# An edge-gated graph layer on one core: GpSimd's queue keeps only fetches and value gathers, SyncE's takes the rest

## The chip, the cores and the metric

The kernel runs on one core of a Trainium2 chip. The metric is the device time of one execution in microseconds (us); the time before is 1040.96 us, the median of three runs (1038.32 to 1042.02).

Names as in the profile: PE is TensorE (matrix products), DVE is VectorE, ACT is ScalarE, POOL is GpSimd, SP is SyncE. SP only issues DMAs. Each engine takes its instructions strictly in the order of the program, so an instruction that waits holds up all that stand behind it on that engine.

## The reference

One layer of a graph network over 16 batches, 1024 nodes and 256 features, with one sparse adjacency matrix for all batches (about 0.8% of entries, and the diagonal):

```python
pre_u = jnp.einsum('bud,dk->buk', h_t, W1[:d])
pre_v = jnp.einsum('bvd,dk->bvk', h_t, W1[d:])
hidden = jax.nn.relu(pre_u[:, :, None, :] + pre_v[:, None, :, :] + b1)
S = jax.nn.sigmoid(jnp.einsum('buvk,ko->buvo', hidden, W2)[..., 0] + b2[0])
a_t = jnp.einsum('buv,bud->bvd', S * A_a, h_t)
m_t = jnp.einsum('uv,bud->bvd', A_m, h_t) * h_t
z_t = beta1 * h_t + beta2 * (a_t @ Wa + ba) + beta3 * (m_t @ Wm + bm)
```

`A_a` and `A_m` are the same matrix `adj`. The last line is shortened from two einsums. Only pairs (u, v) with an edge matter, so the kernel lists the edges and works on these.

## The kernel before, in words

**Blocks and steps.** The 16 batches form four groups of four (`NG`, `GB`). The 1024 target nodes form eight tiles of 128 (`NT`). One group and one tile make a block: 32 blocks, and each is done in ten steps (`T`), so 320 steps in all. Blocks run in a fixed `order`: tiles 0 to 5 of group 0, tiles 0 to 5 of group 1, tiles 6 and 7 of both, then groups 2 and 3. Group 1's table is thus first needed at block 6, by step 60.

**Lists.** For each tile a list of edges is made (`lists(vt)`, line 236). It loads a 128x1024 piece of the adjacency into `key` (line 238), finds the neighbours with DVE's top-8 instruction, computes a matrix of marks on ACT (`mark`, lines 305 to 307), copies it to bytes as `few` (lines 310 and 312), and writes it out with four DMAs to `whose` (line 315), which the blocks read later. It leaves row numbers `uidx` for the fetches and `vidx` for the gathers of edge values. Lists 0 to 3 are made in the opening, the end of list 3 in the first steps; lists 4 to 7 start at steps 7, 14, 44 and 82 and are threaded between the steps' instructions.

**Tables.** For each group a table in device memory holds, for each node, 4x256 values of `pre_u` beside 4x256 values of `h`: 8 KB a row. A piece of rows is made by `rows(k)` (line 429): PE multiplies a transposed tile of x (`hT`, 0.5 MB, `load_hT` at line 400) by `w_u`, ACT copies the result to `tab`, SP writes it to the table. `copy_h` (line 406) copies the `h` half from memory to memory. Group 0's table is made in the opening. Group 1's eight tiles follow in steps that `plan` lists at line 806, two pieces to a tile; `made_rows(n)` (line 813) loads a tile ahead of its first step, when one of the few places in `hT_free` is open, and makes the piece when its step comes.

**A step.** `fetch(n)` (line 513) is an indirect DMA on POOL: 128 edges, one 8 KB table row each, 1 MB in all, into one of eight places (`fetched`). PE spreads `pre_v` over the edges (`expand`, line 616). DVE adds it (`add`, line 646) and, batch by batch, takes the relu, multiplies by W2 and sums (`gate`, line 653). ACT makes the sigmoid (line 656) and scales the edge weights (line 660). PE sums the fetched `h` rows per target (`aggregate`, line 669). Then the place is free and the next fetch is issued, with one or two gathers of edge values (`fetch_val`, line 356), one DMA of 128 numbers each. The products with `Wa` and `Wm` and the output follow at the end of a block.

**The order of the work** is written out by hand. The opening is a `script` (line 544) of 14 short strings: a digit advances that list, `r` makes rows, `h` the first block's `pre_v`, `f` issues the first eight fetches and five value gathers, `w` warms PE up, `m` loads the first mark. After it comes the loop over steps. `after(step, f)` runs `f` at the end of that step. POOL's queue, in the part that matters here, holds: fetches 0 to 7 with five gathers and two `hT` loads among them (in `f`); then `key` of list 4, `w_a`, `w_m`; then the four `whose` writes of list 2; then one `hT` load, the four `whose` writes of list 3, and only then fetch 8.

**Bias.** In step 1 SP loads the biases and the betas; in step 10 `scale_late` (line 598) scales them with seven DVE instructions, and the two weight matrices with two ACT instructions.

Of the kernel before, what the change touches and what calls it, by code (L numbers as in the profile page):

```python
# [11 lines left out]
ALU = mybir.AluOpType  # L12
AX = mybir.AxisListType
P = 128
# [3 lines left out]
def kernel(  # L18
# [42 lines left out]
    nc = tc.nc  # L61
    B, N, D = x.shape
    NT = N // P
    DC = D // P
# [3 lines left out]
    W = 64  # L68
    NW = P // W
# [31 lines left out]
    def fixed(shape, name, dt=FP):  # L101
        return const.tile(shape, dt, name=name)
# [74 lines left out]
    def spread(parts, v):  # L177
        nc.vector.tensor_copy(parts, v)
        nc.vector.tensor_tensor(parts[W:], v[W:], parts[W:].bitcast(FP), ALU.subtract)
        nc.vector.tensor_scalar(parts, parts.bitcast(FP), edge, None, ALU.mult)  # L180

    b1_p = fixed([P, D], "b1_p", FR)
    bias_p = fixed([P, D], "bias_p", FR)
# [5 lines left out]
    whose = const.tile([P, NT * NW, E], mybir.dt.uint8, name="whose")  # L189
# [31 lines left out]
    EARLY = 4  # L221
# [13 lines left out]

    def lists(vt):
        key = fetched[vt + 1][:, :N] if vt < EARLY else lst.tile([P, N], FP, name="key", bufs=1)
        (nc.sync if vt < EARLY else nc.gpsimd).dma_start(key, adjT[vt * P:(vt + 1) * P, :])
        yield "load"
        R = Rs[vt % EARLY]  # L240
        top = R[:, 4:]
# [64 lines left out]
        nc.scalar.activation(mark, mark, AF.Sign, bias=span[:, 0:1], scale=-1.0)  # L306
        nc.scalar.activation(mark, mark, AF.Relu)
        yield "step"
        if vt < EARLY:
            nc.scalar.copy(few, mark)  # L310
        else:
            nc.gpsimd.tensor_copy(few, mark)
        for w in range(NW):
            for h in range(2):
                nc.gpsimd.dma_start(whose[h * W:(h + 1) * W, vt * NW + w, :], few[w * W:(w + 1) * W])
        pe = aside(vt)
        for j in range(TW):
            nc.tensor.matmul(pe[:, j * NW * RC:(j + 1) * NW * RC], mark[:, j * P:(j + 1) * P],
# [54 lines left out]
    def after(step, f):  # L373
        due.setdefault(step, []).append(f)
# [8 lines left out]
    hTs = {}  # L383
# [16 lines left out]
    def load_hT(k, engine=nc.sync):  # L400
        g, nt = k
        hTs[k] = hT_free.pop(0)
        engine.dma_start(hTs[k].rearrange("p b c n -> p (b c) n"),
                         xT_rows[:, g * GB * DC:(g + 1) * GB * DC, nt * P:(nt + 1) * P])
# [95 lines left out]
    T = TW * NW  # L500
# [40 lines left out]
    for i in range(COPIES):  # L541
        copy_h(turn[i], nc.sync)

    script = ("r r 0 0", "r r 1 0 0", "r r 1", "r 0 0", "r r 1", "0 2 r 1", "0 0 r r", "1 2 r 1", "v r r 2", "r 1 3",
              "h 2 1 1", "h 2 2 3", "f 2 2 2 w h h h", "m 3 w 3 3 3")
    begun_rows = {}
    marks, pcs, accs, evs, hbs, LTs, lefts = {}, {}, {}, {}, {}, {}, {}

# [4 lines left out]
    def warm(times):  # L553
        acc = psa.tile([P, 2, D], FP, name="acc")
        for i in range(times):
            nc.tensor.matmul(acc, unit, b1_p.unsqueeze(1).to_broadcast([P, 2, D]), start=True, stop=True)

    m = 0
    piece = None
    parts = halves(0)  # L560
    for t, turns_ in enumerate(script):
        step = t - 100
        do(step)
        for c in turns_.split():
            if c == "r":
                k = turn[m % NT]
                if m < NT:
                    begun_rows[k] = rows(k, tabs[m])
                    next(begun_rows[k])
                go(begun_rows[k], step)  # L570
                if m > NT and m - NT + COPIES <= NT:
                    copy_h(turn[m - NT + COPIES - 1], nc.sync)
                m += 1
            elif c == "h":
                go(parts, step)
            elif c == "v":
                fetch_val(3)
                spread(b1_p, b1_b)
                next(parts)
            elif c == "f":  # L580
                for n in range(NF):
                    fetch(n)
                    if n > 2:
                        fetch_val(1)
                    if n in (3, 6):
                        load_hT(turn[NT + n // 6], nc.gpsimd)
                next(made[EARLY])
                w_a = load_weights(Wa, "w_a", nc.gpsimd)
                w_m = load_weights(Wm, "w_m", nc.gpsimd)
            elif c == "m":  # L590
                load_mark(0)
            elif c == "w":
                warm(6)
            else:
                next(made[int(c)], None)
    do(len(script) - 100)

    def scale_late():
        nc.vector.tensor_scalar(ba_b, ba_b, be2, None, ALU.mult)
        nc.vector.scalar_tensor_tensor(bias, bias, be3, ba_b, ALU.mult, ALU.add)  # L600
        spread(bias_p, bias)
        nc.vector.tensor_scalar(ba_c, ba_c, be2, None, ALU.mult)
        nc.vector.scalar_tensor_tensor(bias_c, bias_c, be3, ba_c, ALU.mult, ALU.add)
        nc.scalar.activation(w_a, w_a, AF.Copy, scale=be2)
        nc.scalar.activation(w_m, w_m, AF.Copy, scale=be3)
        hT_free.append(spare_)

# [192 lines left out]
    def plan(blocks, ns):  # L800

        for k, pieces in zip(blocks, ns):
            pending.append((pieces[0], k))
            at.update((n, k) for n in pieces)

    plan(turn[NT:], ((2, 4), (8, 9), (10, 15), (19, 20), (25, 29), (30, 35), (39, 40), (45, 47)))
    for g, first in ((2, 60), (3, 140)):
        plan([(g, vt) for vt in range(NT)], ((first + 9 + 10 * i, first + 14 + 10 * i) for i in range(NT)))
    pending.extend((order.index(k) * T - T + 1, k) for k in again)
# [2 lines left out]

    def made_rows(n):
        nonlocal piece, last
        while pending and (pending[0][1] in hTs or hT_free and pending[0][0] - AHEAD <= n):
            k = pending.pop(0)[1]
            if k not in hTs:
                load_hT(k, nc.gpsimd if n < T else nc.sync)
        if n in at:
            if at[n] != last:  # L820
                last = at[n]
                copy_h(last, nc.sync)
                piece = rows(last)
                next(piece)
            go(piece, n)
# [58 lines left out]
    for n in range(total - 3):  # L884
        k, s = divmod(n, T)
        if n < ROOM:
            gather_to(n - 1)
        pair_ends()
        if n % TW == (n < ROOM) and n // TW + 1 < total // TW:
            load_mark(n // TW + 1)  # L890
        expand(n + 2)
        if n >= ROOM:
            fill(n, False)
        products(n, k, s)
        if n >= ROOM and n % 2 == 0:
            gather_to(n)
        add(n + 1)
        gate(n)
        while behind:
            nc.scalar.copy(*behind.pop(0))  # L900
        do(n)
        if n == 1:
            bias = load_rows(bm, D, "bias", nc.sync, spare[:, 1])
            ba_b = load_rows(ba, D, "ba_b", nc.sync, spare[:, 2])
            bias_c, ba_c = fixed([P, DC], "bias_c"), fixed([P, DC], "ba_c")
            nc.sync.dma_start(bias_c, bm.rearrange("(c p) -> p c", p=P))
            nc.sync.dma_start(ba_c, ba.rearrange("(c p) -> p c", p=P))
            be1 = load_rows(beta1, 1, "be1", nc.sync)
            be2 = load_rows(beta2, 1, "be2", nc.sync)
            be3 = load_rows(beta3, 1, "be3", nc.sync)  # L910
            after(10, scale_late)
        if n == total - 6:
            hbs[BS - 1] = next(t for t in hT_free if t in flat).rearrange("p b c n -> p b (c n)")
            for v, m, f in tails:
                for h, o in tail_rows(x, v, m, f):
                    nc.sync.dma_start(h, o)
        for i in advance.get(n, ()):
            next(made[i], None)
        if n in start_list:
            running.append([made[start_list[n]], True, n])  # L920
            piece_of(running[-1], n)
        if n < ROOM:
            fill(n, False)
        if n == LISTS:
            assert not running and all(next(x, None) is None for x in made)
            lists_done()
            more = main.enter_context(tc.tile_pool(name="more", bufs=1))
            flat.extend(hT_places(more, MORE, NH))
            hT_free.extend(flat[-MORE:])
            minus.append(more.tile([P, P], FR, name="minus"))  # L930
            nc.vector.tensor_scalar(minus[0], ident, -1.0, None, ALU.mult)
        if n == 120:
            nc.vector.tensor_tensor(rest, rest, taken, ALU.subtract)
            nc.gpsimd.partition_all_reduce(longest, rest, P, bass_isa.ReduceOp.max)
            after(n + 12, count_rest)
# [152 lines left out]
```

## Time and profile before

| what | value |
|---|---|
| median of three runs | 1040.96 us |
| the profiled execution | 1031.14 us, span 1029.3 us |
| DVE busy | 950.4 us (92%) |
| PE busy | 958.9 us (93%) |
| ACT busy | 886.5 us (86%) |
| POOL busy | 467.5 us (45%) |
| moved by DMA | 375.00 MB, mean 364 GB/s |

The span runs from the first to the last of the program's instructions. An engine's idle time is shown before the instruction that ended it, in square brackets, with what it waited for. "remote" means that the profile cannot name the releaser. POOL's DMAs are those of queue 0 (software), SP's those of queue 1 (hardware). The "DMA share" is the mean busy share of the core's 16 DMA engines; as packets of two queues overlap, it can go a little above 1.

### The profile page before, as it was taken

The page shows a single profiled execution, that of the slowest core. Times are in us where ns is not written, and L with a number is a line of the kernel's source. Part 1 is how long each engine was busy: PE and PEld are TensorE (multiplying, and loading weights), DVE is VectorE, ACT ScalarE, POOL GpSimd, SP SyncE. Part 2 cuts the span into 40 slices and gives each one's busy share as a digit, 9 for nine tenths or more (in the row PEclk, how much of TensorE's full clock was granted, in tenths as well). Part 3 has the DMA queues.
Part 4 walks back from the last instruction along what each step waited for, and adds up shares of the span by engine and source line. Part 5 has one row for each costly group of instructions (what it writes and reads, how often), then busy time and mean ns, then how long its engine had stood idle before and what let it go on. Part 6 is the DMA issues. An engine that isn't in the chain of part 4 may idle for free.

```text
span 1029.3 us, 21645 instructions
## 1 busy us (share of the span) xinstructions
PE 958.9 (93%) x6408; PEld 700.3 (68%) x6408; DVE 950.4 (92%) x3302; ACT 886.5 (86%) x2750; POOL 467.5 (45%) x487
## 2 busy tenths in 40 slices
PE   7886789999899999999999999999999999999996
PEld 5754566676567766767677777777777766777663
DVE  7585979988999999998999999999999999999994
ACT  3665777888888989989899999999999999999984
POOL 3367676746246433564333334333343344444430
PEclk9988899999999999999999999999999999999998
DMA  9898998999999999999999999999999999999992
GB/s 326 304 371 305 350 327 287 332 382 343 360 330 334 378 412 392 381 355 391 411 412 408 414 403 413 401 404 408 391 418 390 379 370 364 381 362 378 373 360 73
DMA packets 123199, 375.00 MB, mean 364 GB/s; under 512 B 17616, under 2 KB 76496, under 8 KB 86864
## 3 DMA queue, kind: packets, MB, share of 16 engines
q0 software_dynamic: 50976, 302.73, 76.1%
q1 hardware_dynamic: 71472, 70.27, 20.3%
q8 instruction: 53, 0.87, 0.3%
q10 hardware_dynamic: 624, 0.52, 0.2%
q14 instruction: 74, 0.61, 0.1%
HBM read 377.53 MB, written 50.33 MB: 416 GB/s over the span
## 4 chain that ended last, share of the span: by engine, by line
PE 45%; DVE 28%; issue 12%; ACT 7%; DMA 5%; POOL 2%; another core or an unknown queue 1%; POOLq 0%; DVEq 0%; SPq 0%; ACTq 0%
DVE fetched L653 15%; PE misc L414 13%; DVE fetched L646 11%; PE misc L740 9%; PE pc L616 8%; PE acc L669 8%; PE misc L691 4%; DMA fetched<-table,uidx 3%; ACT left L660 2%; POOL fetched L516 2%; DVE LT L708 1%; PE misc L724 1%; DMA val<-in_adjT_dram,vidx 1%; DMA wide<-in_xT_dram 1%; DVE low L477 1%
## 5 line engine op out<-in xcount | busy, mean ns | idle before, releaser
L516 POOL DMA_INDIRECT fetched<-table,uidx x320 | 342.7, 1071 | 464.6 <-PE acc L669 318.9
L653 DVE SCALAR_TENSOR_TENSOR fetched<-fetched,w_b 128x256 f32<-128x256 f32 x1280 | 476.7, 425 | 0.0
L646 DVE TENSOR_TENSOR fetched<-fetched,pc 128x1024 f32<-128x1024 f32 x320 | 389.8, 1218 | 43.0 <-DMA fetched<-table,uidx 13.8
L660 ACT ACTIVATE left<-left,gt 128x16 f32<-128x16 f32 x1280 | 285.7, 298 | 0.0
L616 PE MATMUL pc<-X,mark 128*128 128x512 f32 x640 | 227.5, 450 | 21.6 <-DVE fetched L646 17.3
L669 PE MATMUL acc<-fetched,left 128*32 128x256 f32 x2560 | 189.9, 388 | 13.0 <-ACT gt L656 4.5
L616 PEld LDWEIGHTS pc<-X,mark 128*128 128x128 f32 x640 | 105.9, 190 | 108.9 <-issue 55.0
L669 PEld LDWEIGHTS acc<-fetched,left 128*32 128x32 f32 x2560 | 74.4, 109 | 92.9 <-issue 30.0
L656 ACT ACTIVATE gt<-sc,b_b 128x4 f32<-128x4 f32 x320 | 96.7, 302 | 39.4 <-DVE fetched L653 31.6
L740 PE MATMUL misc<-w_a,LT 128*128 128x256 f32 x496 | 117.6, 380 | 1.6 <-issue 1.0
L740 PE MATMUL misc<-w_m,LT 128*128 128x256 f32 x496 | 117.3, 380 | 0.0
L653 DVE DVE_READ_ACCUMULATOR fetched<-fetched,w_b 128x1 f32 x1280 | 108.7, 85 | 0.0
L740 PEld LDWEIGHTS misc<-w_a,LT 128*128 128x128 f32 x496 | 93.8, 190 | 16.6 <-issue 1.4
L677 ACT COPY ev<-acc 128x512 f32<-128x512 f32 x160 | 92.2, 577 | 9.8 <-PE misc L414 5.2
L414 PE MATMUL misc<-w_u,wide 128*128 128x256 f32 x384 | 93.4, 392 | 7.2 <-DMA w_u<-in_W_dram 7.1
L624 ACT ACTIVATE left<-onehot,val 128x32 f32<-128x32 bf16 x320 | 99.9, 312 | 0.0
L356 POOL DMA_INDIRECT val<-in_adjT_dram,vidx x80 | 84.9, 1062 | 26.2 <-issue 21.0
L740 PEld LDWEIGHTS misc<-w_m,LT 128*128 128x128 f32 x496 | 89.7, 191 | 9.7
L691 PE MATMUL misc<-ident,ev 128*128 128x128 f32 x642 | 82.8, 274 | 7.1 <-ACT ev L677 3.0
L414 PE MATMUL misc<-w_v,wide 128*128 128x256 f32 x368 | 88.4, 384 | 0.0
L414 PEld LDWEIGHTS misc<-w_u,wide 128*128 128x128 f32 x384 | 74.7, 197 | 19.8 <-DMA w_u<-in_W_dram 7.1
L691 PEld LDWEIGHTS misc<-ident,ev 128*128 128x128 f32 x642 | 74.0, 141 | 17.1 <-ACT ev L677 4.1
(167 smaller groups left out, 1007.6 us busy)
## 6 DMA issues: line engine op xcount, KB each, us to landing
table<-in_x_dram SPq DMA_DIRECT2D x32, 512.0 KB
out_dram<-z SPq DMA_DIRECT2D x62, 256.0 KB
table<-tab SPq DMA_DIRECT2D x48, 256.0 KB
wide<-in_xT_dram SPq DMA_DIRECT2D x16, 512.0 KB
fetched<-table,uidx POOLq DMA_INDIRECT x320
wide<-in_xT_dram SPq DMA_DIRECT2D x4, 1024.0 KB
table<-fetched SPq DMA_DIRECT2D x8, 512.0 KB
hT<-in_xT_dram SPq DMA_DIRECT2D x8, 512.0 KB
```

Of the source, the lines that this page charges most:

```text
L414: nc.tensor.matmul(p[:, bb * D:(bb + 1) * D], hT[:, 2 * h + bb, i, :], wt[:, i, :], start=(i == 0 and not begun), stop=(i == DC - 1), skip ...
L516: nc.gpsimd.indirect_dma_start(out=fetched[at_slot[n]], out_offset=None, in_=table[g], in_offset=bass.IndirectOffsetOnAxis(ap=uidx[:, vt * ...
L616: nc.tensor.matmul(pcs[n][:, c], marks[n // TW][:, j * P:(j + 1) * P], cuts[k][w][:, c], start=True, stop=True)
L624: nc.scalar.activation(lefts[n][:, 1::GB, :], onehot[:, vt * NW + w, j, :].unsqueeze(1).to_broadcast([P, GB // 2, V]), AF.Copy, scale=val[ ...
L646: nc.vector.tensor_tensor(t, t, pcs.pop(n), ALU.add)
L653: nc.vector.scalar_tensor_tensor(t[:, b, :], t[:, b, :], 0.0, w2_b, ALU.max, ALU.mult, accum_out=sc[:, b:b + 1])
L656: nc.scalar.activation(gt, sc, AF.Sigmoid, bias=b2_b)
L660: nc.scalar.activation(lefts[n][:, 2 * b, :], lefts[n][:, 1 + b // 2 * GB, :], AF.Copy, scale=gt[:, b:b + 1])
L669: nc.tensor.matmul(accs[i][b * 2 * V:(b + 1) * 2 * V, r, :], left[:, 2 * b - b % 2:2 * b - b % 2 + 2].rearrange("p k v -> p (k v)"), f[:, ...
L677: nc.scalar.copy(evs[i], accs.pop(i))
L691: nc.tensor.matmul(pt[:, :, FROM[j]:FROM[j] + V], evs[i][:, r, c * P:(c + 1) * P], ident, is_transpose=True, start=(j == of[0]), stop=True ...
L740: nc.tensor.matmul(pz[:, bb * D:(bb + 1) * D], LT[:, 2 * h + bb, i if bb else 1 - i, c, :], wt[:, c, :], start=(i == 1 and bb == 0 and c = ...
```

## The change

All DMAs on POOL but the indirect ones move to SP: `key` of lists 4 to 7, all 32 `whose` writes, the early `hT` loads, `w_a` and `w_m`. The byte copy `few` of lists 4 to 7 moves from POOL to ACT.

The biases and betas are loaded in the opening, at `f`, and scaled at the end of the opening (`scale_bias`, `s` in the script); the spare place that held them is given to `hT_free` there, and not in step 10. The weights are still scaled in step 10.

The first `hT` tile of group 1 is loaded at `k` in the script, the second at the end of step 0, behind the `whose` writes of list 3 and ahead of `key`, `w_a` and `w_m`. Later ones come 6 steps ahead of their first piece while the step is under 10, and 14 steps ahead after that, as before. The pieces themselves fall in steps whose last digit is 1, 3, 8 or 9 (but for the first two, in steps 4 and 6), from step 4 to 41, where they fell in steps 2 to 47.

```diff
-        (nc.sync if vt < EARLY else nc.gpsimd).dma_start(key, adjT[vt * P:(vt + 1) * P, :])
+        nc.sync.dma_start(key, adjT[vt * P:(vt + 1) * P, :])
...
-        if vt < EARLY:
-            nc.scalar.copy(few, mark)
-        else:
-            nc.gpsimd.tensor_copy(few, mark)
+        nc.scalar.copy(few, mark)
         for w in range(NW):
             for h in range(2):
-                nc.gpsimd.dma_start(whose[h * W:(h + 1) * W, vt * NW + w, :], few[w * W:(w + 1) * W])
+                nc.sync.dma_start(whose[h * W:(h + 1) * W, vt * NW + w, :], few[w * W:(w + 1) * W])
...
-              "h 2 1 1", "h 2 2 3", "f 2 2 2 w h h h", "m 3 w 3 3 3")
+              "h 2 1 1", "h 2 2 3", "f 2 2 2 k w h h h", "m 3 w 3 3 3 s")
...
+    def scale_bias():
+        nc.vector.tensor_scalar(ba_b, ba_b, be2, None, ALU.mult)
+        nc.vector.scalar_tensor_tensor(bias, bias, be3, ba_b, ALU.mult, ALU.add)
+        spread(bias_p, bias)
+        nc.vector.tensor_scalar(ba_c, ba_c, be2, None, ALU.mult)
+        nc.vector.scalar_tensor_tensor(bias_c, bias_c, be3, ba_c, ALU.mult, ALU.add)
+        hT_free.append(spare_)
...
                     fetch(n)
                     if n > 2:
                         fetch_val(1)
-                    if n in (3, 6):
-                        load_hT(turn[NT + n // 6], nc.gpsimd)
-                next(made[EARLY])
-                w_a = load_weights(Wa, "w_a", nc.gpsimd)
-                w_m = load_weights(Wm, "w_m", nc.gpsimd)
+                bias = load_rows(bm, D, "bias", nc.sync, spare[:, 1])
...
+            elif c == "k":
+                load_hT(turn[NT])
+            elif c == "s":
+                scale_bias()
...
-    plan(turn[NT:], ((2, 4), (8, 9), (10, 15), (19, 20), (25, 29), (30, 35), (39, 40), (45, 47)))
+    plan(turn[NT:], ((4, 6), (9, 11), (13, 18), (19, 21), (23, 28), (29, 31), (33, 38), (39, 41)))
...
-        while pending and (pending[0][1] in hTs or hT_free and pending[0][0] - AHEAD <= n):
+        while pending and (pending[0][1] in hTs or hT_free and pending[0][0] - (AHEAD if n >= T else 6) <= n):
...
-                load_hT(k, nc.gpsimd if n < T else nc.sync)
+                load_hT(k, nc.sync)
...
+        if n == 0:
+            for i in advance[0]:
+                next(made[i], None)
+            load_hT(turn[NT + 1])
+            next(made[EARLY])
+            w_a, w_m = load_weights(Wa, "w_a", nc.sync), load_weights(Wm, "w_m", nc.sync)
+            after(10, scale_weights)
```

More of the change, by code (lines that the diff above doesn't have):

```diff
@@ L584 @@
                         fetch_val(1)
-                    if n in (3, 6):
-                        load_hT(turn[NT + n // 6], nc.gpsimd)
-                next(made[EARLY])
-                w_a = load_weights(Wa, "w_a", nc.gpsimd)
-                w_m = load_weights(Wm, "w_m", nc.gpsimd)
+                bias = load_rows(bm, D, "bias", nc.sync, spare[:, 1])
+                ba_b = load_rows(ba, D, "ba_b", nc.sync, spare[:, 2])
+                bias_c, ba_c = fixed([P, DC], "bias_c"), fixed([P, DC], "ba_c")
+                nc.sync.dma_start(bias_c, bm.rearrange("(c p) -> p c", p=P))
+                nc.sync.dma_start(ba_c, ba.rearrange("(c p) -> p c", p=P))
+                be1 = load_rows(beta1, 1, "be1", nc.sync)
+                be2 = load_rows(beta2, 1, "be2", nc.sync)
+                be3 = load_rows(beta3, 1, "be3", nc.sync)
+            elif c == "k":
+                load_hT(turn[NT])
+            elif c == "s":
+                scale_bias()
             elif c == "m":
@@ L596, with scale_weights @@
     do(len(script) - 100)
[L598 to L603, printed above, removed]
+    def scale_weights():
         nc.scalar.activation(w_a, w_a, AF.Copy, scale=be2)
         nc.scalar.activation(w_m, w_m, AF.Copy, scale=be3)
-        hT_free.append(spare_)
     def expand(n):
@@ L901 @@
         do(n)
[L902 to L911, printed above, removed]
+        if n == 0:
[5 more added lines that the diff above has]
+            after(10, scale_weights)
         if n == total - 6:
@@ L916 @@
                     nc.sync.dma_start(h, o)
-        for i in advance.get(n, ()):
+        for i in advance.get(n, ()) if n else ():
             next(made[i], None)
```

## The prediction

> **What bounds the kernel now.** I read the page first, then busy time by stretches, then the timelines of DVE, POOL and PE from 50 to 160 us.
>
> ```profile
> span 1029.3 us, 21645 instructions
> PE 958.9 (93%) x6408; PEld 700.3 (68%) x6408; DVE 950.4 (92%) x3302; ACT 886.5 (86%) x2750; POOL 467.5 (45%) x487
> ```
>
> ```profile
> core 0: us, PE busy (x) PEld busy (x) DVE busy (x) ACT busy (x) POOL busy (x), PEclk, DMA share, GB/s
> 58.00:82.27 24.27, 19.11 (x103) 12.39 (x104) 22.28 (x73) 17.27 (x54) 14.48 (x18) 0.93 1.02 387
> 82.27:90.00 7.73, 2.67 (x22) 1.23 (x17) 0.01 (x2) 4.02 (x11) 6.21 (x9) 0.85 0.76 246
> 90.00:112.00 22.00, 14.83 (x68) 10.21 (x68) 15.89 (x51) 7.04 (x24) 15.93 (x17) 0.81 0.95 335
> 112.00:200.00 88.00, 80.33 (x492) 57.63 (x491) 76.72 (x282) 71.09 (x216) 61.53 (x60) 0.94 0.95 326
> 200.00:250.00 50.00, 48.45 (x316) 36.38 (x316) 42.61 (x144) 43.44 (x131) 30.59 (x32) 1.00 0.95 343
> 250.00:300.00 50.00, 42.87 (x292) 29.32 (x291) 49.37 (x174) 43.55 (x137) 21.29 (x23) 1.00 0.96 361
> ```
>
> DVE is idle for 1029.3 - 950.4 = 78.9 us in all. From 58 to 300 us, where the change acts, it is busy for 206.9 of 242 us (the sum of its column), so 35 us are idle there, and these are all that any reordering of these steps can win on DVE. The next column to read is the DMA share: 1 minus the share, times the length, gives the time in which the 16 DMA engines had nothing: 1.9 us from 82.27 to 90, 1.1 to 112, 4.4 to 200, 2.5 to 250, 2.0 to 300, together 11.9 us. So DMA is closer to full than DVE. No byte leaves the program with this change, so if the transfers cost what they cost now, 11.9 us is the most that better filling can give.
>
> The places where DVE waits for data:
>
> ```profile
> 90.00 1.22 DVE L646 TENSOR_TENSOR fetched<-fetched,pc 128x1024 f32<-128x1024 f32 x1 [7.72 <-DMA fetched<-table,uidx]
> 93.84 1.22 DVE L646 TENSOR_TENSOR fetched<-fetched,pc 128x1024 f32<-128x1024 f32 x1 [0.58 <-DMA fetched<-table,uidx]
> 102.86 1.22 DVE L646 TENSOR_TENSOR fetched<-fetched,pc 128x1024 f32<-128x1024 f32 x1 [3.23 <-remote]
> 111.43 1.22 DVE L646 TENSOR_TENSOR fetched<-fetched,pc 128x1024 f32<-128x1024 f32 x1 [2.12 <-remote]
> ```
>
> These are steps 8, 9, 11 and 12; each add can wait only for its fetch or for PE, and as PE had its product ready I read the two "remote" as fetches. Sum: 13.65 us. Why the first came late stands in the timelines of PE and POOL:
>
> ```profile
> 65.89 1.21 PE L669 MATMUL acc<-fetched,left 128*32 128x256 f32 x8 [0.18 <-ACT left L660]
> ```
>
> ```profile
> 67.26 0.95 POOL L403 DMA_DIRECT2D wide<-in_xT_dram  x1
> 68.52 1.09 POOL L516 DMA_INDIRECT fetched<-table,uidx  x1 [0.30 <-issue]
> 71.35 0.60 POOL L238 DMA_DIRECT2D key<-in_adjT_dram  x1
> ...
> 79.87 0.52 POOL L315 DMA_DIRECT2D whose<-few  x1 [2.00 <-DMA val<-in_adjT_dram,vidx]
> 80.42 0.93 POOL L403 DMA_DIRECT2D wide<-in_xT_dram  x1
> 81.91 2.07 POOL L315 DMA_DIRECT2D whose<-few  x4 [0.56 <-ACT left L660]
> 84.29 1.06 POOL L516 DMA_INDIRECT fetched<-table,uidx  x1 [0.30 <-PE misc L691]
> ...
> 97.52 1.00 POOL L516 DMA_INDIRECT fetched<-table,uidx  x1 [0.30 <-issue]
> ```
>
> Fetch 7 is issued at 68.52. Fetch 8 needs place 0, which step 0's sums on PE free at 65.89 + 1.21 = 67.1, yet it is issued at 84.29: 17 us late, because twelve other DMAs stand before it on POOL, some waiting for earlier DMAs to land.
>
> **The change part by part.** *POOL's queue.* With those twelve on SP, fetch 8 follows fetch 7 by one issue: about 70 us, and 9 to 12 follow as places come free. What is late next is the transfer. A fetch is 1 MB; at the 387 GB/s of the stretch 58 to 82.27 it takes 1.05/387 = 2.7 us of all engines. Fetch 7 had landed by 79.67, when step 7's add ran without a wait:
>
> ```profile
> 79.67 1.22 DVE L646 TENSOR_TENSOR fetched<-fetched,pc 128x1024 f32<-128x1024 f32 x1
> ```
>
> So fetch 8 would land by 82.4 at full rate, and at about 85 when SP's loads take a quarter of the engines (below). DVE would be ready at 82.27: of 7.72 us I keep 0 to 3 as a wait. For all four waits the bounds are 0 and 13.65. Inside them the DMA engines decide: to 112 us they had 1.9 + 1.1 = 3.0 us free, and the new plan puts off, past step 12, about one 0.5 MB tile, one 0.5 MB copy of `h` and one 0.25 MB table write, 1.25 MB or 3.7 us at 335 GB/s. So 6.7 us could be won by step 12. The 3.7 must be paid by step 42, and the idle engine time from 112 to 250 us (4.4 + 2.5) can hold it. I take **6 us**, nearer to the DMA bound than to 13.65, because the share is the column closest to full.
>
> *Bias in the opening.* Seven DVE instructions move from step 10 to the end of the opening:
>
> ```profile
> 106.15 0.35 DVE L599 TENSOR_SCALAR hT<-hT,be 128x256 f32<-128x256 f32 x1
> ...
> 108.48 0.22 DVE L603 SCALAR_TENSOR_TENSOR bias_c<-bias_c,be,ba_c 128x2 f32<-128x2 f32 x1
> ```
>
> ```profile
> 58.49 1.22 DVE L646 TENSOR_TENSOR fetched<-fetched,pc 128x1024 f32<-128x1024 f32 x1 [0.81 <-issue]
> 61.00 1.22 DVE L646 TENSOR_TENSOR fetched<-fetched,pc 128x1024 f32<-128x1024 f32 x1 [1.29 <-DMA fetched<-table,uidx]
> ```
>
> They take 106.15 to 108.70, 2.5 us. In the opening 0.81 + 1.29 = 2.1 us of idle time cover them, so 0.4 us shows. SP runs ahead of the other engines there, so the betas have landed; if not, DVE waits with add 0 behind it, up to some 2 us. In step 10 the 2.5 us were followed by a wait of 2.12 for fetch 12, so between 0.4 and 2.5 comes free. Net: a gain of **0.5**, between -2 and +2.
>
> *`few` on ACT.* POOL's copy slowed DVE:
>
> ```profile
> L653 DVE SCALAR_TENSOR_TENSOR fetched<-fetched,w_b 128x256 f32<-128x256 f32 x1280 | 476.7, 425 | 0.0
> ```
>
> ```profile
> 146.90 0.91 POOL L312 CAST few<-made 128x640 uint8<-128x640 f32 x1
> ```
>
> ```profile
> 146.29 0.95 DVE L653 SCALAR_TENSOR_TENSOR fetched<-fetched,w_b 128x256 f32<-128x256 f32 x1
> 147.17 0.92 DVE L653 SCALAR_TENSOR_TENSOR fetched<-fetched,w_b 128x256 f32<-128x256 f32 x1
> 152.96 1.22 DVE L646 TENSOR_TENSOR fetched<-fetched,pc 128x1024 f32<-128x1024 f32 x1 [4.86 <-PE pc L616]
> ```
>
> Two instructions of 425 ns took 0.95 and 0.92: 1.0 us lost, here hidden by the 4.86 us that DVE then waits for PE. Four lists give 0 to 4 us; I take **1**, as only the lists of steps 44 and 82 fall where DVE is nearly full. ACT pays for it:
>
> ```profile
> L310 ACT CAST few<-made 128x640 uint8<-128x640 f32 x4 | 2.9, 724 | 0.0
> ```
>
> That row is ACT's cast of the first four lists: four more cost 2.9 us again, beside 17 us that ACT has free from 112 to 200 alone. Uncovered, 2.9 is lost.
>
> *Rows of group 1.* PE makes the same products, in 38 steps and not 46; PE's free time (7.7 us from 112 to 200, 1.6 to 250) may move either way. I cost it at nothing, within 2 us: group 1's table is first fetched by step 52, and was written in time when its last piece came in step 47. SP's queue now holds list 3's marks, which wait for ACT's cast, ahead of a tile, `key`, `w_a` and `w_m`; none of these is due before step 7 or so.
>
> Sum: 6 + 0.5 + 1 = 7.5; I take off 0.5 for rows and rounding: 7 us. The profiled execution would go from 1031.14 to 1024.1 (span 1022.3). The median of the runs is 9.8 above the profiled execution, and the same 7 us from it gives **1034.0 us**.
>
> **The rivals.** *1, no change: SP's loads take the fetches' time.* Now the loads stand in a queue of their own, and do not wait for the fetches ahead.
>
> ```profile
> q0 software_dynamic: 876, 4.33, 78.5%
> q1 hardware_dynamic: 1624, 1.20, 24.3%
> ```
>
> This is 105 to 120 us: with both queues filled, SP's (q1) gets about a quarter of engine time while POOL's (q0) is never empty. Then fetches 2 to 7 land up to a quarter later (3.4 and not 2.7 us each, 4 us by fetch 7), DVE's new waits come there, and 4 of the 6 us go. With the rest at its lower end the gain is 1: 1040 us. Against it: before, the same loads stood in front of these fetches in POOL's own queue. The Trainium skill, "DMA: Bandwidth & Descriptors", section on queues, rings and completion order, says that each engine goes round the queues packet by packet; the two rows above agree with it, and by that rule alone this rival is what one would expect.
>
> *2, slower: PE waits for a tile that SP loads late.* The second tile is issued behind list 3's marks, and these wait for ACT's cast:
>
> ```profile
> 66.33 0.72 ACT L310 CAST few<-made 128x640 uint8<-128x640 f32 x1
> ```
>
> So it starts at about 67 us. It is due at step 9; step 7's add started at 79.67 and two more steps of some 3 us make about 86 us. Fetch 12 took from 97.52 to 111.43, 13.9 us, under load. That leaves 86 - 67 - 14 = 5 us. If a tile of 1024 pieces of 512 bytes (the shape of the load) takes twice as long, 28 us, PE stops at step 9 for 9 us with the next steps' products behind it; the third tile, issued six steps ahead (some 20 us), stops it for another 8. The 17 less the 7 gained and 1 or 2 of slack: 8 us lost, 1049 us. It decides from a landing time of about 20 us on. Against it: most of the tile loads from 110 us on were SP's already and PE's waits for them were not among the long ones.
>
> **How the numbers follow.** A difference under 0.3% (3.1 us) can't be told from none here. Forecast 0.64, rival 1 0.20, rival 2 0.16. Low end: all 11.9 us of idle DMA time, 2 of the bias and 2 of the cast, 1025. High end: past rival 1 and a small part of rival 2, 1043; some 0.1 lies on each side. Faster 0.64, same 0.20, slower 0.16.
>
> **What would show it.** Right: fetch 8 issued by 72 us, no POOL row between fetch 7 and it but gathers; the wait before add 8 under 3 us; DMA share from 82 to 112 near 1; L653 never at 0.9 us; L599 to L603 before add 0; steps past 300 us as before. Rival 1: waits before adds 2 to 7 and q1 above a quarter from 60 to 85. Rival 2: PE at L414 waiting for `hT` or `wide`. The forecast is wrong if the wait of 7.7 stays, or goes and the stretch to 250 us gives it back.

## The result, and the profile after

| | before | after |
|---|---|---|
| median | 1039.64 us (4 runs, 1035.03 to 1042.02) | 1024.22 us (4 runs, 1019.53 to 1033.33) |
| ratio, 95% interval | | 0.9874 [0.9839, 0.9910] |
| the profiled execution | 1031.14 us | 1026.43 us |
| fetch 8 issued | 84.29 us | 70.59 us |
| DVE idle before add 8 | 7.72 us | 0 |

The kernel became faster by 1.26%, 13 us, where 7 were forecast. Taken from the 1040.96 us of the prediction the ratio gives 1027.8 us, inside the range; the median itself, 1024.22, lies just under its low end. The two profiled executions are only 4.7 us apart, as single executions scatter: the four of the changed kernel took 1019.53, 1022.00, 1026.43 and 1033.33 us, at a mean granted clock of 0.987, 0.988, 0.984 and 0.979. So the size comes from the medians, and the profiles say where.

The top of the page of the changed kernel:

```profile
span 1024.6 us, 21644 instructions
PE 957.0 (93%) x6408; PEld 696.9 (68%) x6408; DVE 948.3 (93%) x3302; ACT 889.0 (87%) x2754; POOL 438.2 (43%) x441
```

Busy times are nearly the same: no engine got less work, but POOL, which has 46 instructions fewer. The stretches show where it changed. These are those of the prediction, for the changed kernel; the last two columns are the DMA share and GB/s:

```profile
core 0: us, PE busy (x) PEld busy (x) DVE busy (x) ACT busy (x) POOL busy (x), PEclk, DMA share, GB/s
58.00:82.27 24.27, 17.64 (x80) 11.63 (x80) 22.30 (x72) 14.57 (x45) 17.36 (x16) 0.79 1.04 387
82.27:90.00 7.73, 4.69 (x32) 2.92 (x32) 4.74 (x18) 3.93 (x11) 5.05 (x6) 1.00 1.02 386
90.00:112.00 22.00, 18.59 (x112) 12.73 (x113) 19.84 (x74) 17.21 (x55) 12.95 (x13) 0.84 1.06 391
112.00:200.00 88.00, 80.83 (x518) 59.79 (x520) 74.52 (x266) 72.91 (x217) 54.41 (x52) 0.98 0.99 343
200.00:250.00 50.00, 46.38 (x298) 32.19 (x287) 41.94 (x144) 42.25 (x134) 27.03 (x26) 1.00 0.96 344
250.00:300.00 50.00, 43.95 (x299) 30.18 (x298) 48.84 (x180) 43.55 (x133) 17.41 (x16) 1.00 0.91 334
```

From 82.27 to 90 the DMA engines go from a share of 0.76 to 1.02 and from 246 to 386 GB/s, to 112 from 335 to 391. Rate times length, summed over the six stretches, gives 82.6 MB before and 85.1 MB after: by 300 us 2.5 MB more have been moved, 7.4 us at 340 GB/s. From 200 us on nothing more is gained (343 and 344 GB/s to 250 us), and from 250 some is given back (361 and 334).

POOL's timeline shows why. Fetch 7, a gather, fetch 8 (line 513 is the fetch, 353 the gather; the added lines shift the numbers):

```profile
67.66 0.99 POOL L513 DMA_INDIRECT fetched<-table,uidx  x1 [1.75 <-issue]
68.95 1.00 POOL L353 DMA_INDIRECT val<-in_adjT_dram,vidx  x1 [0.30 <-issue]
70.59 1.23 POOL L513 DMA_INDIRECT fetched<-table,uidx  x1 [0.64 <-issue]
```

What DVE waits for from 58 to 300 us (total, times, longest), first in the kernel before:

```profile
DVE fetched L646 <- DMA fetched<-table,uidx: 9.6, 3, 7.7
DVE fetched L646 <- PE pc L616: 9.6, 6, 4.9
DVE fetched L646 <- remote: 6.6, 3, 3.2
DVE fetched L646 <- PE acc L669: 4.8, 2, 2.5
```

and after:

```profile
DVE fetched L652 <- PE acc L675: 9.9, 4, 4.9
DVE LT L714 <- ACT LT L424: 8.2, 5, 3.3
DVE fetched L652 <- PE pc L622: 5.6, 8, 1.3
DVE key L245 <- DMA key<-in_adjT_dram: 4.7, 1, 4.7
DVE fetched L652 <- DMA fetched<-table,uidx: 0.3, 1, 0.3
```

The waits for fetches, 9.6 us, are 0.3. The 6.6 us of "remote" were not for fetches, though I had read two of them so (3.23 us before add 11 and 2.12 before add 12). An add first passes a wait instruction for its fetch and then waits for PE. Here is that wait instruction of adds 8, 11 and 12 in the kernel before (its length in ns, and when it ran):

```profile
L646 DVEq EVENT_SEMAPHORE  x1: 21/21/21, 89.9 to 89.9; - x1
L646 DVEq EVENT_SEMAPHORE  x1: 21/21/21, 100.0 to 100.0; - x1
L646 DVEq EVENT_SEMAPHORE  x1: 21/21/21, 108.5 to 108.5; - x1
```

For add 8 it runs at the end of the idle time, so that wait was for the fetch. Adds 11 and 12 start at 102.86 and 111.43, some 3 us after it: their fetches had landed by 100.0 and 108.5, and what was left to wait for was PE. The same holds for the third "remote", before the add at 173.12.

The fourth line of the changed kernel is new, and no step of the prediction has it: DVE stands for 4.7 us before its first work on list 4, for `key`. It is the row of one instruction, and add 9 stands behind it:

```profile
91.74 0.69 DVE L245 SCALAR_TENSOR_TENSOR key<-key,ukey 128x512 f32<-128x512 f32 x1 [4.72 <-DMA key<-in_adjT_dram]
```

SP's timeline has its origin (SPq is SP's queue of DMA issues; the second column is how long the issue itself took, as time that SP waits stands between the rows: the marks start at 69.64, 0.02 us after ACT's cast of them ends):

```profile
69.64 2.38 SPq L312 DMA_DIRECT2D whose<-few  x4
72.12 0.53 SPq L400 DMA_DIRECT2D wide<-in_xT_dram  x1
72.69 2.67 SPq L238 DMA_DIRECT2D key<-in_adjT_dram  x1
...
80.91 8.11 SPq L439 DMA_DIRECT2D table<-tab  x1
```

`key` is issued at 72.69, behind list 3's marks and the second tile, and lands at about 91.7: 19 us for 0.5 MB. On POOL's queue, in before_again (below), it was issued at 71.89 and landed 9.3 us later.

### The profile page after: what moved, and what is told of

It is laid out like the page before. It is cut to its first block, busy times and chain, and to the rows that moved or that the text cites. A ratio compares the mean times of both kernels' runs of the same rounds, so it can differ in the third digit from the quotient of the medians.

```text
span 1024.6 us, 21644 instructions
## 1 busy us (share of the span) xinstructions
PE 957.0 (93%) x6408; PEld 696.9 (68%) x6408; DVE 948.3 (93%) x3302; ACT 889.0 (87%) x2754; POOL 438.2 (43%) x441
## 4 chain that ended last, share of the span: by engine, by line
PE 56%; DVE 23%; ACT 8%; issue 8%; DMA 3%; POOL 1%; another core or an unknown queue 0%; POOLq 0%; DVEq 0%
PE misc L411 16%; DVE fetched L659 11%; PE misc L746 11%; PE pc L622 10%; PE acc L675 9%; DVE fetched L652 8%; PE misc L697 4%; DMA fetched<-table,uidx 3%; ACT left L666 2%; PE misc L730 1%; DVE LT L714 1%; PE misc L415 1%; ACT ev L683 1%; ACT X L906 1%; POOL fetched L513 1%
## 5 line engine op out<-in xcount | busy, mean ns | idle before, releaser
L622 PE MATMUL pc<-X,mark 128*128 128x512 f32 x640 | 229.8, 451 | 20.7 <-DVE fetched L652 11.9
L675 PE MATMUL acc<-fetched,left 128*32 128x256 f32 x2560 | 183.6, 388 | 4.6 <-ACT ev L683 3.1
L675 PEld LDWEIGHTS acc<-fetched,left 128*32 128x32 f32 x2560 | 71.8, 109 | 81.9 <-issue 23.2
L659 DVE DVE_READ_ACCUMULATOR fetched<-fetched,w_b 128x1 f32 x1280 | 99.0, 77 | 0.0
L411 PE MATMUL misc<-w_v,wide 128*128 128x256 f32 x368 | 91.5, 394 | 0.0
```

The costliest lines, as they stand in the source:

```text
L411: nc.tensor.matmul(p[:, bb * D:(bb + 1) * D], hT[:, 2 * h + bb, i, :], wt[:, i, :], start=(i == 0 and not begun), stop=(i == DC - 1), skip ...
L622: nc.tensor.matmul(pcs[n][:, c], marks[n // TW][:, j * P:(j + 1) * P], cuts[k][w][:, c], start=True, stop=True)
L659: nc.vector.scalar_tensor_tensor(t[:, b, :], t[:, b, :], 0.0, w2_b, ALU.max, ALU.mult, accum_out=sc[:, b:b + 1])
L675: nc.tensor.matmul(accs[i][b * 2 * V:(b + 1) * 2 * V, r, :], left[:, 2 * b - b % 2:2 * b - b % 2 + 2].rearrange("p k v -> p (k v)"), f[:, ...
```

## The experiments

Two theories were to be told apart. By the first, the gain is POOL's queue: fetch 8 and those after it no longer stand behind loads and marks. By its rivals it is the new steps of group 1's rows, or the smaller parts (bias, cast), and the queue's gain goes into late loads on SP. The runs came in four groups, each on one chip with the kernel before, whose median there was 1020.12, 1019.87, 1021.06 and 1019.89 us, against 1039.64 on the chip of the result. Ratios are to the kernel before on the same chip, and a gain in us is 1 less the ratio, times that median.

### The change again

Nothing is edited. after_again belongs to the first group, after_third to the third; before_again is one execution of the kernel before, for its profile on a chip like these.

> The changed kernel once more, as the measure for the other three on this chip. Both theories expect 0.987 of the kernel before, within 0.984 to 0.991.

> The changed kernel, as the measure for the other two on this chip: 0.990 to 0.996 of the kernel before.

> The kernel before, for a profile beside the others on this chip. Both theories: 1.0 of itself, fetch 8 issued after 80 us, waits for fetches 8 to 12 of 10 us or more.

Measured: 0.9933 [0.9903, 0.9962], 1012.25 us, and 0.9928 [0.9901, 0.9954], 1013.09 us: a gain of 7 us on both, where the first was expected within 0.984 to 0.991. The three intervals with that of the result just meet at 0.9903 to 0.9910, so that 13 and 7 differ by chip is not shown, nor excluded. before_again's execution took 1016.72 us and has the old wait again, in the same place (its waits for fetches 8 to 12 are 6.89 + 0.52 + 0.54 = 8.0 us, where 10 or more were expected):

```profile
90.03 1.22 DVE L646 TENSOR_TENSOR fetched<-fetched,pc 128x1024 f32<-128x1024 f32 x1 [6.89 <-DMA fetched<-table,uidx]
```

In after_again and after_third the wait for `key` is there again as well, with 7.57 and 5.22 us. What DVE waits for from 58 to 300 us in before_again (nothing is "remote" here):

```profile
DVE fetched L646 <- DMA fetched<-table,uidx: 17.7, 13, 6.9
DVE fetched L646 <- PE pc L616: 3.3, 4, 1.6
```

and in after_again:

```profile
DVE fetched L652 <- PE pc L622: 9.0, 7, 2.5
DVE key L245 <- DMA key<-in_adjT_dram: 7.6, 1, 7.6
DVE fetched L652 <- DMA fetched<-table,uidx: 0.9, 1, 0.9
```

Fetches cost 16.8 us less, but `key` takes 7.6, and the waits for PE and ACT together rise from 3.3 to 11.9. Add 60 starts 5.7 us earlier, 260.8 against 266.5.

### POOL's queue alone, and all but POOL's queue

queue_alone is the kernel before with its direct DMAs moved from POOL to SP, at their old places in the program:

```diff
-        (nc.sync if vt < EARLY else nc.gpsimd).dma_start(key, adjT[vt * P:(vt + 1) * P, :])
+        nc.sync.dma_start(key, adjT[vt * P:(vt + 1) * P, :])
...
-                nc.gpsimd.dma_start(whose[h * W:(h + 1) * W, vt * NW + w, :], few[w * W:(w + 1) * W])
+                nc.sync.dma_start(whose[h * W:(h + 1) * W, vt * NW + w, :], few[w * W:(w + 1) * W])
...
-                        load_hT(turn[NT + n // 6], nc.gpsimd)
+                        load_hT(turn[NT + n // 6])
```

and so with `w_a`, `w_m` and the tiles of the first ten steps. queue_undone is the changed kernel with the same DMAs put back on POOL; bias, cast and steps stay changed:

```diff
-                load_hT(turn[NT])
+                load_hT(turn[NT], nc.gpsimd)
...
-            load_hT(turn[NT + 1])
+            load_hT(turn[NT + 1], nc.gpsimd)
```

and so with `key`, `whose`, `w_a`, `w_m`.

> The kernel before with only the direct DMAs moved from POOL to SP, at their old places in the program; POOL still casts the late lists' marks, bias and rows as before. If POOL's queue is the cause (my theory): fetch 8 issued by 72 us, the wait of 7.7 us before add 8 under 3 us, and at least two thirds of the gain: 0.988 to 0.992. If the rival holds, that rows, bias or the cast bring the gain: 0.996 or more, with new waits for SP's loads in place of the old one.

> The changed kernel with these DMAs back on POOL; bias in the opening, cast on ACT and the new rows stay. If POOL's queue is the cause: fetch 8 issued after 80 us again, a wait of 5 us or more before add 8, and 0.995 to 1.0 of the kernel before. Rival: 0.992 or less.

Measured: queue_alone 0.9924 [0.9897, 0.9951], 1011.38 us, just above the expected range; queue_undone 0.9993 [0.9969, 1.0018], 1018.60 us. The queue alone brings 7.7 us, the same as the whole change on that chip (6.8) within the intervals, and the rest without it brings nothing that can be measured. No run leaves the loads on POOL behind fetch 8, so that their place in the queue is the cause, and not POOL's queue as such, is read from the traces and not tested. In queue_alone's trace fetch 8 follows at 72.48, and add 8 starts without a wait. Nor does DVE wait for `key`, which SP issues there at 48.88, ahead of list 2's marks:

```profile
72.48 0.99 POOL L516 DMA_INDIRECT fetched<-table,uidx  x1 [0.36 <-PE misc L414]
```

```profile
85.68 1.21 DVE L646 TENSOR_TENSOR fetched<-fetched,pc 128x1024 f32<-128x1024 f32 x1
```

(Its profiled execution, span 1019.9 us, loses its time late: from add 200 to add 250 it takes 148.5 us, where after_again takes 137.0. Only its first 100 us are read here.) In queue_undone the loads and marks stand between fetch 7 and fetch 8 again, and fetch 8 comes at 80.94:

```profile
66.92 0.99 POOL L513 DMA_INDIRECT fetched<-table,uidx  x1 [1.73 <-DMA fetched<-table,uidx]
...
80.94 1.07 POOL L513 DMA_INDIRECT fetched<-table,uidx  x1 [0.30 <-issue]
```

Its loss does not lie in one place. The expected wait of 5 us before add 8 is not there, since add 7 before it has waited 4.23 us for PE, and the waits for fetches come in small pieces (58 to 300 us):

```profile
DVE fetched L652 <- DMA fetched<-table,uidx: 8.7, 8, 2.0
```

A fetch that is late by 10 us thus need not show as one wait of 10 us; it is the sum over the stretch that is to be compared, 9.6 and 17.7 us in the two profiles of the kernel before. Waits for PE's products are 11.2 us here, against 3.3 in before_again. This execution (1013.12 us) is the fastest of the twelve of its kernel, so its waits are likely a low reading.

### The steps of group 1's rows

Three kernels go back to the old steps, each from the changed kernel. old_plan has the old steps and the old rule of 14 steps ahead from the start on:

```diff
-    plan(turn[NT:], ((4, 6), (9, 11), (13, 18), (19, 21), (23, 28), (29, 31), (33, 38), (39, 41)))
+    plan(turn[NT:], ((2, 4), (8, 9), (10, 15), (19, 20), (25, 29), (30, 35), (39, 40), (45, 47)))
...
-        while pending and (pending[0][1] in hTs or hT_free and pending[0][0] - (AHEAD if n >= T else 6) <= n):
+        while pending and (pending[0][1] in hTs or hT_free and pending[0][0] - AHEAD <= n):
```

> The changed kernel with the rows of group 1 in their old steps and loaded 14 steps ahead from the start. My theory costs the new steps at nothing: within 2 us of the changed kernel (0.985 to 0.991 of the kernel before). Rival, that the new steps are a part of the gain: 0.993 or more.

Measured: 1.0026 [0.9999, 1.0052], 1022.68 us, so the whole gain is gone, where none of it was expected to go. But the kernel does more than it was meant to: with 14 steps ahead the second tile is loaded in step 0 by the rule and once more by the change's own load, nine tiles for eight, with one place for tiles lost. SP's timeline shows what this does to the queue:

```profile
53.96 15.86 SPq L400 DMA_DIRECT2D wide<-in_xT_dram  x2
69.91 11.09 SPq L312 DMA_DIRECT2D whose<-few  x4
81.10 0.53 SPq L400 DMA_DIRECT2D hT<-in_xT_dram  x1
```

The two loads are the second and the third tile, which the rule of 14 steps brings into step 0 as well; the row at 81.10 is the second tile once more. The issue of the third takes 14.86 of the 15.86 us, and what stands behind it is late. So it settles nothing on the steps. Two kernels without that flaw followed. old_plan_early is old_plan with both first tiles loaded once, at `f`, ahead of the biases and of list 2's marks:

```diff
-              "h 2 1 1", "h 2 2 3", "f 2 2 2 k w h h h", "m 3 w 3 3 3 s")
+              "h 2 1 1", "h 2 2 3", "f 2 2 2 w h h h", "m 3 w 3 3 3 s")
...
+                load_hT(turn[NT])
+                load_hT(turn[NT + 1])
                 bias = load_rows(bm, D, "bias", nc.sync, spare[:, 1])
...
-            load_hT(turn[NT + 1])
```

old_steps is the changed kernel with only the line of `plan` put back.

> The kernel with the rows of group 1 in their old steps, but with the first two tiles issued on SP at the place of the first fetches, ahead of the biases and of list 2's marks. If the old steps cost 9 us because their tiles landed late (my theory, after PE's wait of 2.8 us for a tile that took 20 us to land): no PE wait for a tile in steps 2 to 9, and 0.993 to 0.997 of the kernel before. Rival, that the old steps are bad by themselves with SP's queue as it now is: 1.000 or more.

> The changed kernel with only the line of steps put back (pieces in steps 2 to 47); the tiles are loaded at the changed kernel's places, the first at k, the second behind list 3's marks, the third six steps ahead. In old_plan the second tile went over SP twice, which this kernel avoids. If a tile on SP takes about 20 us to land and that is too long for step 2 (my theory): PE waits 2 to 4 us for the tile there, DVE about as long behind it, and the time is 2 to 5 us over the changed kernel's, 0.995 to 0.998 of the kernel before. Rival, that old_plan's 9 us were the doubled load and the lost place alone: 0.990 to 0.994 with no wait for a tile.

Measured: old_plan_early 0.9921 [0.9893, 0.9949], 1012.74 us; old_steps 0.9946 [0.9919, 0.9974], 1014.95 us. Both times are lower than expected, 0.993 to 0.997 and 0.995 to 0.998. In old_steps PE waits for the first tile, which SP issued at 54.44 and which PE gets at 77.89, for 9.52 us where 2 to 4 were expected, and DVE waits behind it at add 5:

```profile
54.44 0.59 SPq L400 DMA_DIRECT2D hT<-in_xT_dram  x1
```

```profile
77.89 3.78 PE L411 MATMUL misc<-w_u,hT 128*128 128x256 f32 x8 [9.52 <-DMA hT<-in_xT_dram]
```

```profile
86.11 1.22 DVE L652 TENSOR_TENSOR fetched<-fetched,pc 128x1024 f32<-128x1024 f32 x1 [11.76 <-PE pc L622]
```

In old_plan_early the same tile is issued at 45.79, and PE begins at once:

```profile
71.72 1.89 PE L411 MATMUL misc<-w_u,hT 128*128 128x256 f32 x8
```

So the steps by themselves are worth nothing that these runs show: with the tiles in time, the old ones do as well. The new first step, 4 in place of 2, does the same service as an earlier load. The wait of 11.76 us in old_steps makes its ratio only 0.1 to 0.2% higher than those of the two repeats, 1 to 2 us: what comes later has landed by then. Its trace has no wait for `key`, and add 9, at 98.23, is only 4 to 5 us behind the repeats.

### The bias and the cast

bias_late is the changed kernel with the scaling in step 10 again; the biases are still loaded early. few_on_pool has POOL copy `few` for lists 4 to 7 again.

```diff
-              "h 2 1 1", "h 2 2 3", "f 2 2 2 k w h h h", "m 3 w 3 3 3 s")
+              "h 2 1 1", "h 2 2 3", "f 2 2 2 k w h h h", "m 3 w 3 3 3")
...
             after(10, scale_weights)
+            after(10, scale_bias)
```

```diff
-        nc.scalar.copy(few, mark)
+        if vt < EARLY:
+            nc.scalar.copy(few, mark)
+        else:
+            nc.gpsimd.tensor_copy(few, mark)
```

> The changed kernel with the biases scaled in step 10 as before (still loaded in the opening). The prediction gave the move 0.5 us, between -2 and 2: 0.991 to 0.996. If the scaling in the opening delays the first add and everything behind it (rival): the first add 1.5 to 2.5 us earlier and 0.990 or less.

> The changed kernel with the byte copy of the late lists' marks back on POOL. The prediction gave the move 1 us, within 0 to 4, less 2.9 if ACT has no room: so 0.993 to 0.997 here, not to be told from the changed kernel (0.993). Rival, that ACT's four casts cost more than DVE's slower instructions: 0.990 or less.

Measured: bias_late 0.9961 [0.9939, 0.9982], 1016.20 us; few_on_pool 0.9917 [0.9889, 0.9944], 1012.23 us, a little under its expected range. The cast is worth nothing that can be measured, though the mechanism is real; here are the gate instructions (min/median/max ns) of few_on_pool and of the changed kernel:

```profile
L662 DVE SCALAR_TENSOR_TENSOR fetched<-fetched,w_b x1280: 395/414/952, 63.5 to 996.4; 128x256 f32<-128x256 f32 x183
```

```profile
L659 DVE SCALAR_TENSOR_TENSOR fetched<-fetched,w_b x1280: 394/415/496, 63.0 to 1007.8; 128x256 f32<-128x256 f32 x183
```

The longest takes 952 ns beside POOL's copy, and 496 where POOL copies nothing. In few_on_pool three of the four copies each slow one such instruction to 922 or 952 ns, and the fourth none. The Trainium skill, "SBUF — State Buffer", section on who interferes with whom, names the ports that GpSimd shares with DVE as the only ones in contention; the two rows agree, and three such instructions in a whole execution are too little to show in the time.

The bias cost more than forecast when put back: 4.0 us of gain remain out of 7 (6.8 and 7.3 in the other groups, 8.5 for few_on_pool beside it), about 3 us, with intervals that overlap. From add 11 to add 12 bias_late takes 98.53 to 104.78, 6.25 us, where after_again and after_third both take 3.89. So the seven instructions are paid in full there, 2.4 us. In the opening they cost nothing that lasts in these traces: bias_late's first add is 1.0 to 2.1 us earlier than in the two repeats (58.37 against 59.36 and 60.48), as the rival had it, but add 8 is not (83.85 against 83.33 and 84.81), and the time is not lower.

```profile
101.82 0.35 DVE L556 TENSOR_SCALAR hT<-hT,be 128x256 f32<-128x256 f32 x1
...
104.04 0.22 DVE L560 SCALAR_TENSOR_TENSOR bias_c<-bias_c,be,ba_c 128x2 f32<-128x2 f32 x1
104.78 1.22 DVE L652 TENSOR_TENSOR fetched<-fetched,pc 128x1024 f32<-128x1024 f32 x1
```

Against a gain of 3 us stand queue_alone, which scales in step 10 and gains as much as the whole change (it has no wait for `key` either, so the two may cancel), and queue_undone, which has the bias in the opening and gains nothing. The latter would fit if the bias is worth something only once no fetch is waited for after it, but no run tests that by itself, and it stays open.

### The new wait: `key` ahead of the marks

key_first takes the wait away that no step had foreseen: list 4's load goes to the front of what step 0 issues, ahead of list 3's marks and the second tile. key_first_again is the same kernel, beside after_third on one chip.

```diff
         if n == 0:
+            next(made[EARLY])
             for i in advance[0]:
                 next(made[i], None)
             load_hT(turn[NT + 1])
-            next(made[EARLY])
```

> The changed kernel with list 4's adjacency piece issued on SP ahead of list 3's marks and the second tile, instead of behind them. If the wait of 4.7 and 7.6 us for it, seen in two profiles of the changed kernel, takes back a part of what POOL's queue gave (my theory): that wait is gone and the time is 3 to 7 us less than the changed kernel's, 0.986 to 0.990 of the kernel before. Rival, that the DMA engines are the bound there and another wait takes its place: 0.992 to 0.995, with 4 us or more of new waits for fetches or tiles between 80 and 110 us.

> The changed kernel with list 4's adjacency piece issued ahead of list 3's marks, once more, now beside the changed kernel. My theory, that the wait for it costs the changed kernel what one profile pair showed by step 12 (5 to 6 us): 0.986 to 0.990, at least 0.003 under the changed kernel. Rival, that later waits take this back: within 0.002 of it.

Measured: 0.9917 [0.9893, 0.9941], 1012.18 us; again 0.9899 [0.9871, 0.9928], 1012.18 us. SP now issues `key` at 53.85, and DVE no longer waits for it; here is key_first:

```profile
86.80 0.68 DVE L245 SCALAR_TENSOR_TENSOR key<-key,ukey 128x512 f32<-128x512 f32 x1
87.41 1.21 DVE L652 TENSOR_TENSOR fetched<-fetched,pc 128x1024 f32<-128x1024 f32 x1
```

and after_third:

```profile
92.64 0.69 DVE L245 SCALAR_TENSOR_TENSOR key<-key,ukey 128x512 f32<-128x512 f32 x1 [5.22 <-DMA key<-in_adjT_dram]
93.25 1.21 DVE L652 TENSOR_TENSOR fetched<-fetched,pc 128x1024 f32<-128x1024 f32 x1
```

Add 9 starts at 87.41, and at 90.47 in key_first_again, against 93.25 and 94.16 in the two repeats of the change. Both times the wait is gone, and the lead over the changed kernel of the same chip lasts for long: add 60 at 257.5 against 261.0, add 200 at 663.4 against 667.4. A part is taken back at once, as the rival had it: between 80 and 110 us DVE waits 1.9 and 2.2 us for PE and ACT, and PE 2.0 and 3.5 us for a tile. The time does not show the rest: 0.9899 against 0.9928 on the same chip is 0.0029, with intervals that overlap and medians only 0.9 us apart, and the 0.9917 of key_first is also that of few_on_pool, which has the wait. The theory had asked for 3 to 7 us. So the kernel is clearly ahead of the one before, and that it is ahead of the change is not shown.

## Why the prediction was right, point by point

- **POOL's queue** (forecast 6 us, bounds 0 to 13.65): right in mechanism and nearly in size. The upper bound was wrong: 3.23 + 2.12 us of it were waits for PE, as shown above, and the waits for fetches in these steps were 7.72 + 0.58 = 8.3 us. Fetch 8 issued by 72 us: 70.59. Only gathers in front of it: yes. The wait before add 8 under 3 us: none. DMA share near 1 from 82 to 112: 1.02 and 1.06. Alone it measures 7.7 us [5.0, 10.5], and without it nothing measurable is left.
- **The DMA ceiling** (11.9 us of idle engine time): the choice to stay near it, not near the 13.65 us of waits, held. The stretches after it have 0.9 + 2.0 + 4.5 = 7.4 us idle, so 4.5 of the 11.9 were used. But it is no hard ceiling: by 300 us 2.5 MB more had been moved, 7.4 us at 340 GB/s, out of 4.5 us of idle time, as the engines also moved more per share (from 82.27 to 90 us 246 GB/s at 0.76, which is 324 for a full share, against 386 at 1.02, which is 378). The first chip's 13 us lie above the ceiling, but its interval reaches down to 9.4, and the bias is outside it.
- **SP's queue** ("none of these is due before step 7 or so"): the step that failed. It looked up when the moved loads are due and not when they land. `key` is due from step 8 on, just past that mark, and lands 19 us after an issue that itself stands behind the marks: a wait of 4.7 to 7.6 us in all three traces of the change. Rival 2 had the right price (a landing time of 20 us) and the wrong victim: it named PE and the second tile, where DVE and `key` were hit. The row it took its price from was misread: fetch 12, issued at 97.52, had landed by 108.5, so it took at most 11 us and not 13.9.
- **Rival 2** did not come, as the first pieces fall in steps 4 and 9. old_steps shows its mechanism: a tile that lands after 23.5 us stops PE for 9.52 and DVE for 11.76 us.
- **Rival 1** did not come. SP's part of the engines' time from 60 to 85 us rose, but stayed under a quarter. The rows give packets, MB and the share of 16 engines, before:

```profile
q0 software_dynamic: 1900, 8.31, 89.1%
q1 hardware_dynamic: 816, 1.05, 11.9%
```

and after:

```profile
q0 software_dynamic: 1485, 8.22, 83.9%
q1 hardware_dynamic: 2041, 1.42, 19.7%
```

  The 8.31 MB of POOL's queue before held up to 2.4 MB of direct loads and marks; the 8.22 after are fetches and gathers alone, seven fetches issued against four. So the fetches lost nothing, they gained, and adds 2 to 7 have no wait for one in this trace (0.87 us before add 3 in after_third). The Trainium skill, "DMA: Bandwidth & Descriptors", section on queues, rings and completion order, has each engine go round its queues packet by packet. Equal turns would give equal packet counts while both queues are filled; the rows have 1485 and 2041, and those of the prediction 876 and 1624, so that they agree with the rule, as the prediction says, is not shown. The queue that paid for the sharing was SP's, whose few loads landed late.
- **Bias** (forecast 0.5, between -2 and +2): the same sign, and about 3 us in the one run that takes it out, which is past the upper bound. The working let the 2.5 us in step 10 be eaten by the wait of 2.12 us before add 12. That wait was for PE and not for fetch 12, and neither before_again nor the changed kernel has one there. What the 3 us are beyond the 2.4 is open.
- **Cast** (forecast 1, between 0 and 4): no gain measured. **Rows** (forecast nothing, within 2 us): held, by old_plan_early.
- **The start from the profiled execution**: the later groups centre on the 7 us of the forecast (6.8 and 7.3 for the change, 7.7 for the queue alone). The 13 us of the first chip, whose executions took 2% longer before the change too, are not explained. That the sum comes out at 7 is in part luck: the 6 was taken between bounds of which the upper was misread, the cast gave nothing, and the 4.7 to 7.6 us that DVE waits for `key` were in no term.
- **Past 300 us** nothing was to change, and there the first pair misleads. In it the gain shrinks: add 20 starts at 138.8 before and 128.7 after, add 60 at 279.5 and 272.2, add 200 at 688.8 and 683.7. On the other chips it does not: from before_again to after_again and after_third, add 20 is earlier by 4.2 and 5.2 us, add 60 by 5.7 and 5.5, add 200 by 4.5 and 6.7. What the forecast had not foreseen, as it named the DMA engines alone as what is late next, is that DVE then waits for PE and ACT: 3.3 us in before_again, 11.9 and 9.9 in after_again and after_third. In the first pair these waits were long already, 9.6 + 4.8 us with names and 6.6 without, and are 9.9 + 8.2 + 5.6 = 23.7 after.

## What to carry to other kernels

A queue that feeds the bottleneck should hold nothing that can wait on something else; look for the transfer that is issued long after its place is free, and read what stands between. A wait whose releaser the profile cannot name is not to be put down to the suspect: look where the wait instruction for it ran. When loads move to another queue, write down for each not only when it is due, but what stands ahead of it there and how long such a load takes to land under the new load, and put the first one due in front. Read the gain from the sum of a stretch: a late transfer can show as many small waits on other engines, and one long wait can be worth little.

## What the runs showed of the hardware

Beside a filled fetch queue a 0.5 MB load on SP's queue landed after 19 us (`key`, 72.69 to 91.7), 23 us (`hT` in old_steps, 54.44 to 77.9) or 28 us (`key` in key_first_again, issued at 55.12); at the 387 GB/s of that stretch its bytes alone are 1.4 us. The same load of `key` on POOL's own queue, in before_again, took 9.3 us. And SP's issues, mostly about half a microsecond, took up to 8.11 us (a table write at 80.91 in the changed kernel) and 15.86 us (two tile loads in old_plan), so that whatever stood behind them on SP was late before it began.
